# Column sums of three context blocks by accumulating transfers, in float16

## The chip, the core and the metric

The kernel runs on one core of a Trainium2 chip. The core has a matrix engine (TensorE, PE in the profile, with its weight loads as PEld), a vector engine (VectorE, DVE), a scalar engine (ScalarE, ACT), a general engine (GpSimd, POOL) and a queue engine (SyncE, SP). Each runs its own instructions in order, and they wait for each other by semaphores. Sixteen DMA engines move data between the device memory (DRAM), the on-chip buffers and, in this change, from one on-chip buffer to another; SP, ACT and POOL issue such transfers. The metric is the device time of one execution in microseconds (us), lower is better.

## The reference, cut to what matters

```python
# x: (2, 1024, 2048); ctx: (2, 2048, 2048)
def fake_quant(v, s, z):
    q = jnp.clip(jnp.round(v / s + z), 0, 255)
    return (q - z) * s

x = x + jnp.matmul(fake_quant(layernorm(x), s1, z1), fake_quant(ctx, s2, z2))
x = x + ffn(layernorm(x))     # x @ kernel + bias, and two low-rank adapters
```

The kernel keeps the quantised values as whole numbers less 128, which have eight significant bits, and multiplies those. The zero points z1 and z2 need not be 128, so the product has to be corrected by a term with the row sums of the first factor and by a term with the column sums of the second. The column sums of the context, 2048 rows added up for each of 2048 columns, are what this change is about.

## The kernel before, in words

The two batches are worked one after the other. In each, the context is taken in four blocks of 512 columns (n = 0 to 3), and x in four groups of 256 tokens (g = 0 to 3). A pair (b, n, g) is one block times one group: 2 halves of 128 tokens by 16 products of 128x128 by 128x512, accumulated in a bank of PSUM (class Pair, L513). Before its products a pair's bank is filled by ScalarE with the correction, from the block's column term colt[n] and the row sums (begin, L523); after them VectorE scales the bank into y (end, L545) and takes the statistics for the next norm (stats, L549, into st2).

A block's context arrives in eight slices of 256 rows. For each slice (quantise, L451) ScalarE rounds it to int16 (round_ctx, L455), and VectorE clips it, takes off 128 and writes it in two bytes an element into one of the two buffers of c2 (centre_ctx, L463). When all eight are there, column_term (L474) makes the block's column term: column_parts multiplies each of the sixteen 128-row pieces with a 128x32 matrix of ones, four lots of 32 rows of one PSUM tile (pcp), column_copy takes that to an on-chip buffer on VectorE, column_mean sums the 128 rows by one f32 product with a constant matrix (pc), and column_end turns it into colt on VectorE.

The first batch begins with an entry, in an order written out by hand (STEPS, in which u, p, c and v are the parts of the column term). It covers the products of blocks 0 and 1, and the making of block 2. Everything behind the entry is emitted in program order and put in order on each engine by a planner with its own costs. Block 3 of the first batch is quantised while block 2 is multiplied, and its column term is emitted after the third pair of block 2 (L1056 to L1064). In the second batch, blocks 0 and 1 are prepared inside the first batch's feed-forward part. Block 2 goes into the buffers of block 0 when the last pair of block 0 is done; it is quantised and summed while the last pair of block 1 runs (L1042 to L1049). Block 3 goes into the buffers of block 1 and is treated as in the first batch. Three buffers q2b pass the int16 slices from ScalarE to VectorE; ten buffers lit take the loads from DRAM, which SP issues as buffers come free.

After the attention part the adapters' matrices are gated (pg_a, pg_b), and the feed-forward part runs as a two-level fast matrix product with f32 operands on PE, with sums of operands on VectorE and POOL. POOL issues two transfers per batch (L679); the rest of its work is in the feed-forward part.

Of the kernel before, what the change touches and what calls it, by code (L numbers as in the profile page):

```python
# [9 lines left out]

F32 = mybir.dt.float32
BF16 = mybir.dt.bfloat16
U8 = mybir.dt.uint8
I16 = mybir.dt.int16
AF = mybir.ActivationFunctionType
ALU = mybir.AluOpType
# [4 lines left out]
P = 128  # L21
# [4 lines left out]
QMAX = 255.0  # L26
CENTRE = 128.0
# [52 lines left out]
EARLY = [(0, 0), (1, 0), (2, 0)]  # L80
ROWS_ON_SCALAR = ()
PLACED_BY_SCALAR = (2, 3, 4, 5, 6, 7)


class Bufs:
# [13 lines left out]
def tile_quant_xattn_then_lora_ffn(  # L99
# [17 lines left out]
    nc = tc.nc  # L117
# [28 lines left out]
    lit = Bufs([const.tile([P, KQ, GT], F32, tag=f"lit{i}", name=f"lit{i}") for i in range(10)])  # L146
    q2b = Bufs([const.tile([P, 2, NB], I16, tag=f"q2b{i}", name=f"q2b{i}") for i in range(3)])

    acat = const.tile([P, KT, GPB // 2 * 3, R], F32, tag="acat", name="acat")
    own_col = [0, 2, 3, 5]  # L150

# [2 lines left out]
    axT = const.tile([P, GPB // 2, GT], F32, tag="axT", name="axT")  # L154
    gmat = const.tile([P, 2, GPB // 2, RC], F32, tag="gmat", name="gmat")
    st1 = const.tile([P, MT, NN, 6], F32, tag="st1", name="st1")
    st2 = const.tile([P, MT, NN, 6], F32, tag="st2", name="st2")
    r_s = const.tile([P, MT], F32, tag="r_s", name="r_s")

    zs = [  # L160
# [6 lines left out]

    def bf(t, n):

        return t.rearrange("p k n -> p (k n)").bitcast(BF16).rearrange("p (k n) -> p k n", n=n)  # L170

    def flat(t):
        return t.rearrange("p k n -> p (k n)")
# [91 lines left out]
    load_x(0, 3)  # L265
    ahead[0] = 10
    load_next()
    gate_b = const.tile([P, GB, NL], F32, tag="gate_b", name="gate_b")
    nc.sync.dma_start(
        out=gate_b.rearrange("p b n -> p (b n)"), in_=gate.rearrange("b n -> (b n)").partition_broadcast(P)  # L270
    )
# [23 lines left out]

    ident = const.tile([P, P], F32, tag="ident", name="ident")
    make_identity(nc, ident)
    ident_h = const.tile([P, P], BF16, tag="ident_h", name="ident_h")
    nc.gpsimd.tensor_copy(ident_h, ident)
    ones_h = const.tile([P, P], BF16, tag="ones_h", name="ones_h")  # L300
    nc.gpsimd.memset(ones_h, 1.0)


    zeros_h = const.tile([P, P], BF16, tag="zeros_h", name="zeros_h")
    nc.gpsimd.memset(zeros_h, 0.0)
    mean_w = const.tile([P, P], F32, tag="mean_w", name="mean_w")
    nc.gpsimd.memset(mean_w, 1.0 / 32)

# [8 lines left out]

    def gate_values():

        m_ad = const.tile([P, NL], F32, tag="m_ad", name="m_ad")  # L320
        nc.vector.tensor_reduce(m_ad, ident.rearrange("p (n r) -> p n r", r=RC), AX.X, ALU.add)
        nc.vector.tensor_reduce(m_rk, ident.rearrange("p (n r) -> p r n", r=RC), AX.X, ALU.add)
        nc.vector.tensor_tensor(gate_b, gate_b, m_ad.unsqueeze(1).to_broadcast([P, GB, NL]), ALU.mult)
        for b in range(B):
            for i in range(2):
                nc.vector.tensor_reduce(
                    gval[:, ds(b * GPB + i * 2, 2)], gate_b[:, b * GPB + i : (b + 1) * GPB : 2, :], AX.X, ALU.add
                )
# [37 lines left out]
    class XTile:  # L366


        def __init__(self, b, m, c1T, wk):
            self.b, self.m, self.nm = b, m, f"{b}_{m}"  # L370
            self.on_vector = b == 0 and m not in ROWS_ON_SCALAR
            g, tok = m // MG, ds((m % MG) * P, P)
            self.y = y[g][:, m % MG, :]

            wf = flat(wk)
            self.q8 = wf[:, ds((m % 2) * (D // 4), D // 4)].bitcast(U8)
            self.qh = wf[:, D // 2 : D].bitcast(BF16)
            self.to = [c1T[g][:, ds(h * KH, KH), tok] for h in range(2)]
            self.pt = [None, None]

# [37 lines left out]
            )  # L418

        def turn(self, h):  # L420
            self.pt[h] = ps_m.tile([P, KH, P], BF16, tag="pm", name=f"pt_{self.nm}_{h}")
            for kt in range(KH):
                nc.tensor.transpose(self.pt[h][:, kt, :], self.qh[:, ds(h * H + kt * P, P)], ident_h)

# [23 lines left out]
            x.place(h)  # L448
        x.total()

    def quantise(c2, r):  # L451

        centre_ctx(c2, r, round_ctx())

    def round_ctx():  # L455
        buf, t = next_loaded(1)
# [3 lines left out]
        load_next()  # L460
        return qi

    def centre_ctx(c2, r, qi):  # L463
        nc.vector.tensor_scalar(c2[r // 4][:, ds(2 * (r % 4), 2), :], qi, QMAX, CENTRE, ALU.min, ALU.subtract)
        q2b.give(qi)

    def take_c2():
        bufs = [big.take() for _ in range(2)]
        return bufs, [bf(t, NB) for t in bufs]

    colt = {}
    pairs = []

    def column_term(b, n, c2):  # L474

        of = column_parts(b, n, c2)
        column_copy(of)
        column_mean(b, n, of)
        column_end(n, of)

    def column_parts(b, n, c2):

        parts = ps_m.tile([P, NB], F32, tag="pm", name=f"pcp_{b}_{n}")
        for k in range(KT):
            row = P // 4 * (k % 4)
            nc.tensor.matmul(
                parts[row : row + P // 4, :],
                ones_h[:, 0 : P // 4],
                c2[k // 8][:, k % 8, :],
                start=(k < 4),  # L490
                stop=(k >= KT - 4),
                skip_group_check=True,
            )
        return [parts]
# [18 lines left out]
    class Pair:  # L513
# [35 lines left out]
        def stats(self):  # L549
            for j in range(MG):  # L550
                nc.vector.bn_stats(  # L551
                    st2[:, self.g * MG + j, self.n, :], y[self.g][:, j, ds(self.n * NB, NB)]
                )

    def xattn_pair(b, n, g, c1T, c2):
# [66 lines left out]
    def prep_z(b, m, zq, wk):  # L622

        nm = f"{b}_{m}"
        g, tok = m // MG, ds((m % MG) * P, P)
        mean, rstd = norm_stats(st2[:, m], f"z{nm}")
        for h, t in enumerate(halves(wk)):
            nc.vector.tensor_scalar(t, y[g][:, m % MG, ds(h * H, H)], mean, rstd, ALU.subtract, ALU.mult)
            for u in range(2):
                pt = ps_m.tile([P, KQ, P], F32, tag="pm", name=f"ptz_{nm}_{h}_{u}")  # L630
                for k in range(KQ):
                    nc.tensor.transpose(pt[:, k, :], t[:, ds((4 * u + k) * P, P)], ident)  # L632
                nc.scalar.copy(zq[2 * h + u][:, :, tok], pt)
# [288 lines left out]
    def entry():  # L922

        X = [XTile(0, m, c1T, wk) for m in range(MT)]
        qi, parts, at, ad = {}, {}, {}, {}
        idle = ps_acc.tile([P, MG, NB], F32, tag="delta", name="idle")
        recent = [(idle, 0)]
        tick = const.tile([P, 1], BF16, tag="tick", name="tick")

        def pair(n, g):  # L930
            if (n, g) not in at:
# [1 line left out]
            return at[n, g]  # L933

        def products(n, g, j, first, last=None):
            recent.append((pair(n, g).pa, j))
            for r in range(first, (first if last is None else last) + 1):
                pair(n, g).products(j, range(2 * r, 2 * r + 2))

# [16 lines left out]
        def centred(r):  # L956
            if r // NR not in c2:
                next_block(0)
            centre_ctx(c2[r // NR], r % NR, qi.pop(r))

        def sums(n):
            parts[n] = column_parts(0, n, c2[n])

        def keep_busy(n):

            to, j = recent[-1]
            for i in range(n):
                nc.tensor.matmul(
                    to[:, j, :],
                    zeros_h,  # L970
                    (tick if to is idle else ones_h[:, 0:1]).to_broadcast([P, NB]),
                    start=(to is idle),
                    stop=True,
                    skip_group_check=True,
                )

        run = {
            "S": lambda m, n: X[m].stats(n),
# [9 lines left out]
            "Q": rounded,  # L988
            "V": centred,
            "u": sums,  # L990
            "p": lambda n: column_copy(parts[n]),
            "c": lambda n: column_mean(0, n, parts[n]),
            "v": lambda n: column_end(n, parts[n]),
            "B": lambda n, g, j: pair(n, g).begin(j),
            "M": products,
# [6 lines left out]
            "h": ad_copy,  # L1002
            "i": ad_turn,
            "j": lambda n: lora_a_place(n, ad[n]),
            "z": keep_busy,
        }
        for step in STEPS.split():
            done = run[step[0]](*(int(v) for v in step[1:].split(".") if v))
# [11 lines left out]
    for b in range(B):  # L1020
# [9 lines left out]
        else:  # L1030
# [5 lines left out]
            for g in range(2, GPB):  # L1036
                for m in range(g * MG, (g + 1) * MG):
                    with tc.issue_after(opened.ins):
                        prep_x(b, m, c1T, wk)
                for n in range(2):  # L1040
                    xattn_pair(b, n, g, c1T, c2[n])
                    if g + 1 == GPB:  # L1042
                        next_block(n)
                        if n == 0:
                            for r in range(NR):
                                quantise(c2[2], r)
                                if r % 4 == 3:
                                    lora_a_step(b, r // 4)
                            column_term(b, 2, c2[2])  # L1049
# [6 lines left out]
        for g in range(GPB):  # L1056
            if (b, g) != (0, 0):
                xattn_pair(b, 2, g, c1T, c2[2])
            for r in {0: range(3), 1: range(3, 6), 2: range(6, 8), 3: ()}[g]:
                quantise(c2[3], r)  # L1060
            if 1 <= g <= 2:
                lora_a_step(b, g + 1)
            if g == 2:
# [53 lines left out]
        def meanwhile(o, s):  # L1117
# [23 lines left out]
                load_x(nb, m, slice(half * H, (half + 1) * H))  # L1141
            if s < 4:
                for r in range(2 * s, 2 * s + 2):
                    quantise(c2[0], r)
            if 1 <= s <= 4:
                prep_x(nb, s - 1, state["c1T"], state["wk"])
            if s == 3:
# [2 lines left out]
                c2[1] = [bf(c2b[1][0], NB)]  # L1150
            if s == 4:
                for r in range(2):
                    quantise(c2[1], r)
                c2b[1].append(big.take())
                c2[1].append(bf(c2b[1][1], NB))
            if s == 5:
                for r in range(2, 5):
                    quantise(c2[1], r)
            if s == len(INNER) - 1:
                for r in range(5, NR):  # L1160
                    quantise(c2[1], r)
                column_term(nb, 1, c2[1])
                state["c1b"] += [big.take() for _ in range(2)]
                state["c1T"] = [bf(t, GT) for t in state["c1b"]]
# [59 lines left out]
```

## Time and profile before

| | |
|---|---|
| median of 3 runs | 1082.93 us (1082.42 to 1084.54) |
| the profiled execution | 1082.56 us, its span 1080.8 us |
| granted clock of PE | 1.00 |
| DVE, ACT and POOL busy | 71%, 23%, 23% of the span |
| DMA | 257.15 MB, 238 GB/s on average |
| the chain that ended last | PE 83%, DVE 8%, DMA 4%, ACT 3% |

Lines of the profile name an engine, a line of the kernel, an operation, and out<-in by the names of the tiles. L486 is the thin product of the column sums, L505 their f32 mean, L530 the products of a pair, L464 VectorE's write of a slice, L679 a transfer that POOL or ACT issues. An f32 product of the program is two records of PE. "DMA to landing" is the time from the start of the issuing instruction to the last of the 16 semaphore steps of its transfer. A DMA share of 1.00 means that the sixteen engines have packets in work all the time (it can come out a little above). The time in brackets behind an instruction is how long its engine was idle before it, and what ended that.

### The profile page before, as it was taken

How to read it: one execution, taken by the hardware profiler on the slowest of the kernel's cores; microseconds unless marked ns; L12 is line 12 of the kernel's file. 1: busy time of each engine (PE TensorE's matmuls, PEld its weight loads, DVE VectorE, ACT ScalarE, POOL GpSimd, SP SyncE). 2: the span in 40 equal slices, each digit the busy share in tenths (PEclk: the TensorE clock that was granted, in tenths of full speed). 3: DMA queues.
4: the chain of work that ended last, by engine and by line, in shares of the span. 5: the costliest groups of instructions: out<-in, count | busy, mean ns of one | idle time of the engine just before them, and what ended most of it. 6: DMA issues, size and time to landing. Idle time of an engine off the chain costs nothing.

```text
span 1080.8 us, 10609 instructions
## 1 busy us (share of the span) xinstructions
PE 1054.6 (98%) x3932; PEld 489.8 (45%) x3932; DVE 766.6 (71%) x949; ACT 247.4 (23%) x351; POOL 253.8 (23%) x104
## 2 busy tenths in 40 slices
PE   5999999999999999999999999999999999999998
PEld 2443345544444444444444444554444444444443
DVE  7986867578877676677859655674969667756851
ACT  5866133210000000001675741331000000000000
POOL 0000003032435302533000000032244531253600
PEclk9999999999999999999999999999999999999999
DMA  9979645788798476699673292559889874748611
GB/s 341 381 196 308 190 176 190 256 316 295 263 339 324 160 264 217 191 372 321 230 246 119 98 266 103 198 210 360 294 269 297 288 269 148 264 146 301 214 39 58
DMA packets 119228, 257.15 MB, mean 238 GB/s; under 512 B 11272, under 2 KB 15496, under 8 KB 118152
## 3 DMA queue, kind: packets, MB, share of 16 engines
q1 hardware_dynamic: 98688, 215.05, 58.4%
q10 hardware_dynamic: 20168, 40.38, 10.7%
q0 software_dynamic: 320, 1.05, 0.4%
q8 instruction: 31, 0.51, 0.2%
q14 instruction: 21, 0.17, 0.1%
HBM read 220.79 MB, written 37.75 MB: 239 GB/s over the span
## 4 chain that ended last, share of the span: by engine, by line
PE 83%; DVE 8%; DMA 4%; ACT 3%; issue 1%; SPq 0%; ACTq 0%
PE fu L828 34%; PE fv L828 17%; PE pa L530 12%; PE fw L828 9%; PE pl L694 3%; PE px L648 3%; PE ptz L632 2%; DMA lit<-in_ctx_dram 2%; DVE st L551 2%; DVE st L383 1%; ACT q2b L458 1%; DVE y L547 1%; ACT big L412 1%; DVE big L771 1%; PE pg_b L574 1%
## 5 line engine op out<-in xcount | busy, mean ns | idle before, releaser
L828 PE MATMUL fu<-big,lit 128*128 128x512 f32 x896 | 395.3, 593 | 0.0
L828 PEld LDWEIGHTS fu<-big,lit 128*128 128x128 f32 x896 | 168.6, 190 | 206.3 <-issue 204.9
L530 PE MATMUL pa<-big,big 128*128 128x512 bf16 x1024 | 237.1, 381 | 7.3 <-ACT pa L526 3.4
L771 POOL TENSOR_TENSOR lit<-lit,lit 128x1024 f32<-128x1024 f32 x56 | 164.7, 2950 | 189.7 <-PE fw L828 74.6
L828 PE MATMUL fv<-big,lit 128*128 128x512 f32 x448 | 197.9, 594 | 0.0
L771 DVE TENSOR_TENSOR big<-big,big 128x2048 f32<-128x2048 f32 x56 | 164.4, 2935 | 0.7
L530 PEld LDWEIGHTS <-big 128*128 128x128 bf16 x1024 | 97.1, 98 | 136.3 <-issue 29.6
L762 POOL TENSOR_TENSOR lit<-lit,lit 128x1024 f32<-128x1024 f32 x32 | 85.7, 2677 | 256.4 <-DMA lit<-zs 230.4
L852 DVE TENSOR_TENSOR y<-y,fu 128x1024 f32<-128x1024 f32 x92 | 108.5, 1215 | 40.6 <-PE fu L828 40.2
L828 PEld LDWEIGHTS fv<-big,lit 128*128 128x128 f32 x448 | 84.3, 190 | 105.0 <-issue 104.7
L458 ACT ACTIVATE q2b<-lit,sc,inv 128x1024 int16<-128x1024 f32 x64 | 76.4, 1232 | 163.7 <-DMA lit<-in_ctx_dram 147.1
L852 DVE TENSOR_TENSOR y<-y,fv 128x1024 f32<-128x1024 f32 x48 | 56.8, 1218 | 78.8 <-PE fv L828 78.8
L762 DVE TENSOR_TENSOR big<-big,big 128x2048 f32<-128x2048 f32 x40 | 101.8, 2546 | 0.0
L828 PE MATMUL fw<-big,lit 128*128 128x512 f32 x224 | 99.4, 592 | 0.0
L683 ACT COPY pl<-bias 128x1024 f32<-128x1024 f32 x16 | 16.3, 1018 | 294.1 <-DVE y L705 258.1
L679 POOL DMA_DIRECT2D bp<-bd x4 | 2.6, 660 | 344.3 <-DMA bd<-q2b 166.3
L852 DVE TENSOR_TENSOR y<-y,fw 128x1024 f32<-128x1024 f32 x24 | 28.4, 1218 | 53.9 <-PE fw L828 53.9
L828 PEld LDWEIGHTS fw<-big,lit 128*128 128x128 f32 x224 | 42.1, 190 | 50.7 <-issue 50.7
L547 DVE SCALAR_TENSOR_TENSOR y<-pa,k_s,y 128x1024 f32<-128x1024 f32 x32 | 41.0, 1280 | 32.2 <-PE pa L530 32.1
L526 ACT ACTIVATE pa<-bp,r_s 128x512 f32<-128x512 f32 x58 | 39.0, 685 | 87.0 <-PE pa L530 57.1
L705 DVE TENSOR_TENSOR y<-pl,y 128x512 f32<-128x512 f32 x64 | 39.8, 679 | 17.5 <-PE pl L694 17.2
L383 DVE BATCH_NORM_STATS2 st<-y 128x6 f32<-128x512 f32 x64 | 41.4, 679 | 5.7 <-DMA y<-in_x_dram 5.6
(93 smaller groups left out, 629.6 us busy)
## 6 DMA issues: line engine op xcount, KB each, us to landing
big<-in_w_dram SPq DMA_DIRECT2D x96, 1024.0 KB
lit<-zs SPq DMA_DIRECT2D x80, 512.0 KB
lit<-in_ctx_dram SPq DMA_DIRECT2D x64, 512.0 KB
out_dram<-y ACTq DMA_DIRECT2D x30, 512.0 KB
zs<-lit ACTq DMA_DIRECT2D x24, 512.0 KB
lit<-in_lora_a_dram SPq DMA_DIRECT2D x32, 256.0 KB
lit<-in_lora_bt_dram SPq DMA_DIRECT2D x32, 256.0 KB
y<-in_x_dram SPq DMA_DIRECT2D x16, 512.0 KB
```

Source lines behind the costliest of these rows:

```text
L383: nc.vector.bn_stats(st1[:, self.m, n, :], self.y[:, ds(n * NB, NB)])
L458: nc.scalar.activation(qi, t, AF.Relu, bias=z2, scale=inv2)
L526: nc.scalar.activation(self.pa[:, j, :], colt[self.n], AF.Identity, bias=r_s[:, m : m + 1])
L530: nc.tensor.matmul(self.pa[:, j, :], self.c1T[:, k, ds(j * P, P)], self.c2[k // 8][:, k % 8, :], start=not self.begun[j], stop=(k == KT - ...
L547: return nc.vector.scalar_tensor_tensor(yp, self.pa, s12, yp, ALU.mult, ALU.add)
L648: nc.tensor.matmul(px[i * 2 * R : (i + 1) * 2 * R, :], acat[:, k, ds(3 * pr + i, 2), :].rearrange("p s r -> p (s r)"), zqs[i][k // KQ][:, ...
L694: nc.tensor.matmul(pl[j][i][:, half], axT[rows, pr, ds(j * P, P)], bt[rows, half], start=False, stop=True, skip_group_check=True,)
L705: line(nc.vector.tensor_add(yb, pl[j][i], yb))
L762: line(eng.tensor_tensor(got[0], got[0], got[1], ALU.add if terms[1][2] > 0 else ALU.subtract))
L771: line(eng.tensor_tensor(out_t, at[p], at[q], op))
L828: nc.tensor.matmul(ps[m], at[:, k, ds(m * P, P)], bt[:, k, :], start=(opens and k == 0), stop=(ends and k == KQ - 1), skip_group_check=True,)
L852: line(nc.vector.tensor_tensor(yp, yp, whole[chain], op))
```

## The change: what it does

For three of the eight blocks, (b, n) = (0, 3), (1, 2) and (1, 3), the column sums are made in another way. After VectorE has written a slice, GpSimd issues a transfer of that slice (128 partitions x 1024 elements of two bytes, 256 KB) into a new buffer cs: a plain one for the first slice, accumulating ones for the other seven. There is one such buffer. When the eight are in, PE multiplies the two halves of cs with a 128x128 matrix of ones, two products 128x512 into one PSUM tile, and the column term follows from that as before. The sixteen thin products, the copy and the f32 mean of these three blocks are gone.

All two-byte tiles go from bfloat16 to float16, in which the sums of eight values are exact. To make room, the gate table and a small mask use the memory of cs before it is needed, and the second norm's statistics use the same tile as the first's (st1). A tile of zeros and a step that no order calls (keep_busy) are removed.

```diff
-BF16 = mybir.dt.bfloat16
+F16 = mybir.dt.float16
+SUMMED_BY_DMA = ((0, 3), (1, 2), (1, 3))
...
+    cs = Bufs([const.tile([P, 2, NB], F16, tag=f"cs{i}", name=f"cs{i}") for i in range(1)])
...
-    st2 = const.tile([P, MT, NN, 6], F32, tag="st2", name="st2")
...
-    gate_b = const.tile([P, GB, NL], F32, tag="gate_b", name="gate_b")
+    gate_b = cs.spare[0].rearrange("p k n -> p (k n)").bitcast(F32)[:, 0 : GB * NL].rearrange("p (b n) -> p b n", n=NL)
...
-    zeros_h = const.tile([P, P], BF16, tag="zeros_h", name="zeros_h")
-    nc.gpsimd.memset(zeros_h, 0.0)
...
-    def centre_ctx(c2, r, qi):
-        nc.vector.tensor_scalar(c2[r // 4][:, ds(2 * (r % 4), 2), :], qi, QMAX, CENTRE, ALU.min, ALU.subtract)
+    def centre_ctx(b, n, r, qi):
+        part = c2[n][r // 4][:, ds(2 * (r % 4), 2), :]
+        nc.vector.tensor_scalar(part, qi, QMAX, CENTRE, ALU.min, ALU.subtract)
         q2b.give(qi)
+        if (b, n) in SUMMED_BY_DMA:
+            if r == 0:
+                slices[n] = cs.take()
+                nc.gpsimd.dma_start(out=slices[n], in_=part)
+            else:
+                nc.gpsimd.dma_start(out=slices[n], in_=part, accum_op=ALU.add)
...
     def column_term(b, n, c2):
         of = column_parts(b, n, c2)
-        column_copy(of)
-        column_mean(b, n, of)
+        if (b, n) not in SUMMED_BY_DMA:
+            column_copy(of)
+            column_mean(b, n, of)
         column_end(n, of)
 
     def column_parts(b, n, c2):
+        if (b, n) in SUMMED_BY_DMA:
+            pc = ps_m.tile([P, NB], F32, tag="pm", name=f"pc_{b}_{n}")
+            for i in range(2):
+                nc.tensor.matmul(pc, ones_h, slices[n][:, i, :], start=(i == 0), stop=(i == 1))
+            cs.give(slices.pop(n))
+            return [pc]
...
-                    st2[:, self.g * MG + j, self.n, :], y[self.g][:, j, ds(self.n * NB, NB)]
+                    st1[:, self.g * MG + j, self.n, :], y[self.g][:, j, ds(self.n * NB, NB)]
```

More of the change, by code (lines that the diff above doesn't have):

```diff
@@ L168, in bf @@
     def bf(t, n):
-        return t.rearrange("p k n -> p (k n)").bitcast(BF16).rearrange("p (k n) -> p k n", n=n)
+        return t.rearrange("p k n -> p (k n)").bitcast(F16).rearrange("p (k n) -> p k n", n=n)
     def flat(t):
@@ L297, in tile_quant_xattn_then_lora_ffn @@
     make_identity(nc, ident)
-    ident_h = const.tile([P, P], BF16, tag="ident_h", name="ident_h")
+    ident_h = const.tile([P, P], F16, tag="ident_h", name="ident_h")
     nc.gpsimd.tensor_copy(ident_h, ident)
-    ones_h = const.tile([P, P], BF16, tag="ones_h", name="ones_h")
+    ones_h = const.tile([P, P], F16, tag="ones_h", name="ones_h")
     nc.gpsimd.memset(ones_h, 1.0)
-    zeros_h = const.tile([P, P], BF16, tag="zeros_h", name="zeros_h")
-    nc.gpsimd.memset(zeros_h, 0.0)
     mean_w = const.tile([P, P], F32, tag="mean_w", name="mean_w")
@@ L318, in gate_values @@
     def gate_values():
-        m_ad = const.tile([P, NL], F32, tag="m_ad", name="m_ad")
+        m_ad = cs.spare[0].rearrange("p k n -> p (k n)").bitcast(F32)[:, ds(GB * NL, NL)]
         nc.vector.tensor_reduce(m_ad, ident.rearrange("p (n r) -> p n r", r=RC), AX.X, ALU.add)
@@ L376, in __init__ @@
             self.q8 = wf[:, ds((m % 2) * (D // 4), D // 4)].bitcast(U8)
-            self.qh = wf[:, D // 2 : D].bitcast(BF16)
+            self.qh = wf[:, D // 2 : D].bitcast(F16)
             self.to = [c1T[g][:, ds(h * KH, KH), tok] for h in range(2)]
@@ L420, in turn @@
         def turn(self, h):
-            self.pt[h] = ps_m.tile([P, KH, P], BF16, tag="pm", name=f"pt_{self.nm}_{h}")
+            self.pt[h] = ps_m.tile([P, KH, P], F16, tag="pm", name=f"pt_{self.nm}_{h}")
             for kt in range(KH):
@@ L449, in prep_x, with quantise @@
         x.total()
-    def quantise(c2, r):
-        centre_ctx(c2, r, round_ctx())
+    def quantise(b, n, r):
+        centre_ctx(b, n, r, round_ctx())
     def round_ctx():
@@ L471, in tile_quant_xattn_then_lora_ffn @@
     colt = {}
+    slices = {}
     pairs = []
@@ L625, in prep_z @@
         g, tok = m // MG, ds((m % MG) * P, P)
-        mean, rstd = norm_stats(st2[:, m], f"z{nm}")
+        mean, rstd = norm_stats(st1[:, m], f"z{nm}")
         for h, t in enumerate(halves(wk)):
@@ L925, in entry @@
         qi, parts, at, ad = {}, {}, {}, {}
-        idle = ps_acc.tile([P, MG, NB], F32, tag="delta", name="idle")
-        recent = [(idle, 0)]
-        tick = const.tile([P, 1], BF16, tag="tick", name="tick")
+        tick = const.tile([P, 1], F16, tag="tick", name="tick")
         def pair(n, g):
@@ L935, in products @@
         def products(n, g, j, first, last=None):
-            recent.append((pair(n, g).pa, j))
             for r in range(first, (first if last is None else last) + 1):
@@ L958, in centred @@
                 next_block(0)
-            centre_ctx(c2[r // NR], r % NR, qi.pop(r))
+            centre_ctx(0, r // NR, r % NR, qi.pop(r))
         def sums(n):
             parts[n] = column_parts(0, n, c2[n])
[L964 to L975, printed above, removed]
         run = {
@@ L990, in entry @@
             "u": sums,
-            "p": lambda n: column_copy(parts[n]),
-            "c": lambda n: column_mean(0, n, parts[n]),
+            "p": lambda n: (0, n) in SUMMED_BY_DMA or column_copy(parts[n]),
+            "c": lambda n: (0, n) in SUMMED_BY_DMA or column_mean(0, n, parts[n]),
             "v": lambda n: column_end(n, parts[n]),
@@ L1004, in entry @@
             "j": lambda n: lora_a_place(n, ad[n]),
-            "z": keep_busy,
         }
@@ L1045, in tile_quant_xattn_then_lora_ffn @@
                             for r in range(NR):
-                                quantise(c2[2], r)
+                                quantise(b, 2, r)
                                 if r % 4 == 3:
@@ L1059, in tile_quant_xattn_then_lora_ffn @@
             for r in {0: range(3), 1: range(3, 6), 2: range(6, 8), 3: ()}[g]:
-                quantise(c2[3], r)
+                quantise(b, 3, r)
             if 1 <= g <= 2:
@@ L1143, in meanwhile @@
                 for r in range(2 * s, 2 * s + 2):
-                    quantise(c2[0], r)
+                    quantise(nb, 0, r)
             if 1 <= s <= 4:
@@ L1152, in meanwhile @@
                 for r in range(2):
-                    quantise(c2[1], r)
+                    quantise(nb, 1, r)
                 c2b[1].append(big.take())
@@ L1157, in meanwhile @@
                 for r in range(2, 5):
-                    quantise(c2[1], r)
+                    quantise(nb, 1, r)
             if s == len(INNER) - 1:
                 for r in range(5, NR):
-                    quantise(c2[1], r)
+                    quantise(nb, 1, r)
                 column_term(nb, 1, c2[1])
```

## The prediction

> **What bounds the kernel now.** I read the page first, then TensorE (PE) in order of time where the three changed blocks are summed, then the engines that feed it, and last the only transfers that GpSimd (POOL) issues.
>
> ```profile
> span 1080.8 us, 10609 instructions
> PE 1054.6 (98%) x3932; PEld 489.8 (45%) x3932; DVE 766.6 (71%) x949; ACT 247.4 (23%) x351; POOL 253.8 (23%) x104
> ```
>
> PE is busy in 98% of the span and carries 83% of the chain that ended last. So work taken off PE is time gained, and a wait put in front of PE is time lost, one for one. Now the order of PE in the second batch, where block 2 is summed (columns: start, duration, engine, line, operation, count):
>
> ```profile
> 616.62 3.63 PE L530 MATMUL pa<-big,big 128*128 128x512 bf16 x16
> 620.30 0.63 PE L600 MATMUL pga<-ident,q2b 128*128 128x128 f32 x4
> 620.86 1.05 PE L486 MATMUL pcp<-big,ones_h 128*32 128x512 bf16 x16
> 621.84 1.04 PE L530 MATMUL pa<-big,big 128*128 128x512 bf16 x4
> 622.71 1.12 PE L505 MATMUL pc<-q2b,mean_w 128*128 128x512 f32 x2
> 623.67 7.50 PE L530 MATMUL pa<-big,big 128*128 128x512 bf16 x34
> ```
>
> The sixteen thin products (pcp) and the f32 mean (pc) lie in an unbroken row of products; nothing there waits. When the data comes is seen on VectorE (DVE), whose writes at L464 put the eight slices of block 2 in place:
>
> ```profile
> 612.27 0.86 DVE L464 TENSOR_SCALAR big<-q2b 128x1024 bf16<-128x1024 int16 x2 [1.61 <-PE pa L530]
> ...
> 618.47 1.08 DVE L464 TENSOR_SCALAR big<-q2b 128x1024 bf16<-128x1024 int16 x3
> ...
> 620.19 0.43 DVE L464 TENSOR_SCALAR big<-q2b 128x1024 bf16<-128x1024 int16 x1
> ```
>
> The last slice is ready at 620.6, and PE sums at 620.86: hardly any slack. The first slice is ready at 612.7 and cannot be earlier, since it overwrites a buffer that PE has just finished with. The nearest row to the new transfers is bp<-bd, the four DMAs that POOL issues, of 256 KB each, which is also the size of one slice:
>
> ```profile
> L679 POOL DMA_DIRECT2D bp<-bd x1: 686/686/686, 153.8 to 153.8; - x1
> ...
> DMA to landing us min/median/max: 6.9/6.9/6.9
> ...
> L679 POOL DMA_DIRECT2D bp<-bd x1: 852/852/852, 167.4 to 167.4; - x1
> ...
> DMA to landing us min/median/max: 3.9/3.9/3.9
> ...
> DMA to landing us min/median/max: 7.1/7.1/7.1
> ...
> DMA to landing us min/median/max: 4.2/4.2/4.2
> ```
>
> The four answers are in order of time (issued at 153.8, 167.4, 684.2, 698.2). Stretches of the trace (span; sum; PE, PEld, DVE, ACT, POOL; clock; DMA share; GB/s) tell why they differ:
>
> ```profile
> 154.00:161.00 7.00, 7.00 (x38) 2.71 (x36) 3.71 (x10) 1.19 (x4) 0.47 (x1) 1.00 0.97 360
> 168.00:172.00 4.00, 4.00 (x28) 2.40 (x28) 2.04 (x6) 2.16 (x4) 0.25 (x1) 1.00 0.70 220
> ...
> 108.00:121.00 13.00, 12.60 (x63) 5.42 (x62) 13.00 (x24) 0.94 (x2) 0.00 (x0) 1.00 1.04 270
> ...
> 620.00:650.00 30.00, 29.72 (x156) 12.70 (x155) 15.88 (x31) 14.53 (x17) 0.00 (x0) 1.00 1.02 263
> 650.00:660.00 10.00, 10.00 (x62) 4.14 (x61) 5.36 (x10) 1.91 (x3) 0.00 (x0) 1.00 0.02 5
> ```
>
> The third was issued at a share of 1.03, the fourth at 0.53 (stretches 683 to 685 and 697 to 699). With the DMA engines full at the issue a POOL transfer took 7.0 us, otherwise 4.05 (means of two each). The stretches that matter are full: 94 to 121 (block 3 of the first batch) and 614 to 650 (blocks 2 and 3 of the second).
>
> **The change part by part.**
>
> *Taken off PE.* Per block the sixteen thin products take 0.98 us (620.86 to 621.84) and the f32 mean 0.96, 0.96 and 0.86 in the three places (to the next start): together 5.7. Added are two products 128x512, 0.22 each (a row of 32 takes 7.01): 1.3. Gain 4.4 us, all on PE's path. The three copies of 0.69 us leave DVE, which has idle time there: nothing.
>
> *The chain of transfers.* A block has one plain transfer and seven accumulating ones, all into the single buffer cs. In the built program each waits for the semaphore of the one before, so eight times issue-to-landing lie end to end, and PE's two products wait for the last. PE is in order; behind them stand the adapter product pg_a or the running pair, and every pair that needs this column sum. POOL has no other work there (0.00 busy in those stretches), so nothing else is late on it; SP's loads of adapters, which wait for buffers that pg_a frees, are used only behind the same wait. The bounds of one link: below, the trace excludes nothing down to POOL's own issue (0.54 to 0.85 us in the four rows); above, 8.1 full and 5.15 light, if reading the destination doubles the transfer itself, which for queue 0 is 0.4% of the span for four, 1.1 us each. I take 7.0 and 4.05: same issuer, same size, with a plain copy's HBM trip standing in for the second read.
>
> *Second batch, block 2.* Without the old sums PE does 0.56 of pga from 620.30 and sixteen products (3.5), and is at the two products at 624.4. Links: 612.7 to 616.75 light (the loads only start again at 613), five full ones to 651.75, two light ones to 659.85. The loads do not stop with PE: the sixteen rounded slices free their buffers on ScalarE, without PE. Wait 659.85 - 624.4 = 35.4. After it the sum is turned into the bias (DVE 0.81, ACT 0.69, about 1.4 from product to bias, as from 655.35 to 656.7 in this trace) with only pg_a (1.0) in front of the pair: 0.4 more.
>
> *Second batch, block 3.* Its slices are ready by then, but its first transfer stands on POOL behind the other block's and needs cs, so it starts when PE has read cs, 660.3. Eight light links end 32.4 later. PE gets there 24.6 after (24.2 from 626.3 to 650.53 now, and the 0.4): wait 7.8.
>
> *First batch, block 3.* First slice ready at 94.1, four full links to 122.1, four light ones to 138.3; the last slice is written only at 122.46, behind DVE's statistics, and does not decide. PE arrives at 126.2 (pga at 125.20, then two products): wait 12.1. Loads and weights that run meanwhile are waited for by nobody earlier than now.
>
> *The clock after a wait.* The trace has one idle stretch of this kind, 8.0 us before 13.14, and the products after it:
>
> ```profile
> 16.39 1.89 PE L530 MATMUL pa<-big,big 128*128 128x512 bf16 x4 [2.22 <-DVE big L428]
> ...
> 30.41 1.02 PE L530 MATMUL pa<-big,big 128*128 128x512 bf16 x4 [0.23 <-DVE big L464]
> ```
>
> The same four products took 1.89 and later 1.02. Two groups of four and two of eight transposes lost 0.87, 0.72, 0.41 and 0.44 against their later rows: 2.4 us before the pace was reached (bounds: 0, and 2.4). The granted clock says 1.00 all through, so it does not show this. Three waits of about 8 us or more: 7.2.
>
> *Priced at nothing.* float16 for bfloat16 has the same two bytes; the rows that come nearest, bf16 products at 0.22 and weights at 98 ns (f32: 190), I take over. The other end, the f32 product's 0.88, would add hundreds of us and is not credible. The gate table in cs is long used by 94. st1 in place of st2 adds order only among DVE's own instructions, which are in order. zeros_h is a 0.20 us memset on POOL at 1.42, 11 us ahead of the first transpose. keep_busy is called by no step.
>
> *Sum.* 35.4 + 0.4 + 7.8 + 12.1 + 7.2 - 4.4 = +58.5, against this execution's own 1082.56 (span 1080.8), which is 0.4 below the median of 1082.93. Forecast 1141.
>
> *The skill against the rows.* The Trainium skill, "DMA: Bandwidth & Descriptors" (Anatomy of one DMA), puts a transfer from GpSimd at about 2.0 us plus the bytes over 436 GB/s, which makes an estimate of 2.6 us for 256 KB. The four rows of this trace show 3.9 to 7.1, so the rows decide; with 2.6 a link only block 2 of the second batch would wait, and the time would be some 1090. "TensorE: Matmul & The Clock Gate" (Part 1) says that an idle window of about 3.4 us halves the array's clock until as long a busy one has passed. That speaks against a change that makes PE wait; the products after 13.14 agree, and by the page each wait would cost an estimated 1.7 us, the sum being 2 us lower.
>
> **The rivals.**
>
> *A: the queue is no matter.* Without HBM at either end every link takes 4.05. Then 94.1 + 32.4 ends with the last slice (122.9 + 4.05), wait 0.8; block 2 waits until 645.1, 20.7; block 3 7.8; two slow starts 4.8: +30, 1113. For it: the light rows. Against: 6.9 and 7.1 whenever the engines were full.
>
> *B: the second read costs.* 8.1 and 5.15 a link: waits of 20.9, 41.3 and 16.6, in all +82, 1165. For it: twice the bytes are read. Against: no HBM trip.
>
> *C: faster.* The accumulating transfers from buffer to buffer are short. With a link of L, block 2 waits 8L - 11.7; with 0.4 and the gain of 4.4 the balance is at L = 1.96. At 1.46 or less no wait is left, and the time is 1079. For it: PE's gain is real, and no row shows such a transfer. Against: the shortest of four rows is 3.9.
>
> *D: the transfers are hidden in part.* Links of 2.5 to 3.2 give +6 to +13, 1089 to 1096, all of it from block 2 of the second batch.
>
> **How the numbers follow.** A measurement of this kernel tells about 0.2% (2 us) from no change. Forecast 48%, A 22%, B 18%, D 6%, C 4%, and 2% for a link close to 1.96, within 0.2%. Faster 0.04, same 0.02, slower 0.94. The range takes in A (down to links of about 3.8, less slow starts) and reaches past B's 1165: 1104 to 1168; outside it lie C, D and the far side of B.
>
> **What would show it.** On PE, two waits for a DMA of cs before pc in the second batch, 35 and 8 us, and one of 12 in the first; on POOL, 24 transfers, each issued when the one before landed, 7 us apart before 650 and 4 after; on PE 48 records fewer (per block 18 go and 2 come). Products just after the long wait near 0.43 us each. It is wrong if links are shorter than 3.5 us while the engines are full, or if the float16 products are not at 0.22.

## The result, and the profile after

The changed kernel takes 1144.68 us (median of 4 runs, 1141.6 to 1146.71) against 1083.74 before (4 runs). The ratio is 1.0555, with a 95% interval of 1.0522 to 1.0589: it is 61 us slower. The forecast was 1141. The profiled execution took 1141.6 us, its span 1139.7; it is the fastest of the four, 3.1 us below their median, and everything read from the trace below is of this execution.

The page of the kernel after, first lines and the row of TensorE's granted clock:

```profile
span 1139.7 us, 10576 instructions
...
PE 1056.9 (93%) x3884; PEld 489.7 (43%) x3884; DVE 762.8 (67%) x946; ACT 247.7 (22%) x351; POOL 268.5 (24%) x127
...
PEclk9999799999999999999999758999999999999999
...
q0 software_dynamic: 3584, 7.34, 3.3%
```

PE has 48 records fewer, as forecast. PE's busy time does not fall with them (1056.9 us, 1054.6 before), because some of the others now run at a lower clock: the slices where the clock row dips are the ones that hold the three waits. The transfers of GpSimd's queue (q0) are 6.3 MB more than before, 2% of all bytes.

PE in order of time around the three sums, in the kernel after (start, duration, engine, line, operation, count, idle time before):

```profile
139.62 1.04 PE L494 MATMUL pc<-cs,ones_h 128*128 128x512 f16 x2 [14.36 <-DMA cs<-big]
140.45 3.71 PE L544 MATMUL pa<-big,big 128*128 128x512 f16 x12
...
673.29 1.03 PE L494 MATMUL pc<-cs,ones_h 128*128 128x512 f16 x2 [35.16 <-DMA cs<-big]
674.25 1.94 PE L588 MATMUL pg_a<-lit,gmat 128*32 128x512 f32 x8
676.12 11.66 PE L544 MATMUL pa<-big,big 128*128 128x512 f16 x48
...
707.24 1.03 PE L494 MATMUL pc<-cs,ones_h 128*128 128x512 f16 x2 [7.06 <-DMA cs<-big]
708.07 5.76 PE L544 MATMUL pa<-big,big 128*128 128x512 f16 x16
```

The three waits are 14.4, 35.2 and 7.1 us, 56.6 together. Behind each wait the products are slow for a while: the twelve from 140.45 take until 144.09 where 2.63 us is their usual time, the sixteen from 708.07 take until 713.76, 5.7 us instead of 3.5. In the stretch from 707 to 714 PE's granted clock is 0.61. Against the usual times (0.22 us for a product, 1.0 for pg_a) the rows shown lose 1.4, 2.35 and 2.6 us, 6.3 in all. So 56.6 - 4.4 + 6.3 = 58.5, and the spans differ by 58.9. Nothing is given back later: the adapters' products px of the second batch start at 699.8 before and at 758.7 after, 58.9 later, and that difference stays to the end.

The chain itself, on POOL, second batch:

```profile
626.48 0.56 POOL L469 DMA_DIRECT2D cs<-big  x1 [95.38 <-DVE big L464]
632.45 0.90 POOL L471 DMA_DIRECT2D cs<-big  x1 [5.41 <-DVE big L464]
641.58 0.87 POOL L471 DMA_DIRECT2D cs<-big  x1 [8.24 <-DVE big L464]
650.32 0.86 POOL L471 DMA_DIRECT2D cs<-big  x1 [7.87 <-DMA lit<-in_lora_bt_dram]
658.48 0.86 POOL L471 DMA_DIRECT2D cs<-big  x1 [7.30 <-issue]
662.26 0.87 POOL L471 DMA_DIRECT2D cs<-big  x1 [2.92 <-DMA cs<-big]
...
674.62 0.57 POOL L469 DMA_DIRECT2D cs<-big  x1 [3.84 <-PE pc L494]
677.46 0.86 POOL L471 DMA_DIRECT2D cs<-big  x1 [2.27 <-DVE q2b L604]
684.32 0.86 POOL L471 DMA_DIRECT2D cs<-big  x1 [6.00 <-DMA cs<-big]
```

From issue to issue an accumulating link of block 2 takes 8.2 to 9.1 us until 658, then 3.8. (The releasers named are those of the last semaphore that came; the slices were there long before, the last of block 2 at 634.1.) Three stretches of the same kernel (span; sum; PE, PEld, DVE, ACT, POOL; clock; DMA share; GB/s), the second of which lies within the first, show what changes at 658:

```profile
627.00:658.00 31.00, 10.96 (x57) 4.67 (x54) 12.71 (x30) 15.21 (x14) 2.67 (x4) 0.72 1.05 298
650.30:658.50 8.20, 0.00 (x0) 0.00 (x0) 0.00 (x0) 0.00 (x0) 0.88 (x2) 0.50 1.01 280
658.00:674.00 16.00, 0.71 (x2) 0.13 (x2) 0.00 (x0) 0.00 (x0) 3.48 (x4) 0.50 0.40 72
```

The DMA engines are full up to 658 and at 0.40 after it. From 650.3 to 673 PE, VectorE and ScalarE do nothing, with PE's clock granted at half. The link from 650.32 to 658.48 took 8.2 us all the same, and those behind it 3.8: so the length of a link does not come from what VectorE or ScalarE do beside it.

### The profile page after: what moved, and what is told of

The parts are those of the page before. It is cut to its first block, busy times and chain, and to the rows that moved or that the text cites. A ratio compares the mean times of both kernels' runs of the same rounds, so it can differ in the third digit from the quotient of the medians.

```text
span 1139.7 us, 10576 instructions
## 1 busy us (share of the span) xinstructions
PE 1056.9 (93%) x3884; PEld 489.7 (43%) x3884; DVE 762.8 (67%) x946; ACT 247.7 (22%) x351; POOL 268.5 (24%) x127
## 5 line engine op out<-in xcount | busy, mean ns | idle before, releaser
L544 PE MATMUL pa<-big,big 128*128 128x512 f16 x1024 | 240.6, 386 | 6.6 <-ACT pa L540 2.8
L785 POOL TENSOR_TENSOR lit<-lit,lit 128x1024 f32<-128x1024 f32 x56 | 162.8, 2917 | 188.0 <-PE fw L842 60.0
L544 PEld LDWEIGHTS <-big 128*128 128x128 f16 x1024 | 98.5, 99 | 138.3 <-issue 33.6
L776 POOL TENSOR_TENSOR lit<-lit,lit 128x1024 f32<-128x1024 f32 x32 | 82.5, 2580 | 263.3 <-DMA lit<-zs 237.7
L494 PE MATMUL pc<-cs,ones_h 128*128 128x512 f16 x6 | 3.1, 620 | 56.6 <-DMA cs<-big 56.6
```

Source lines behind the costliest of these rows:

```text
L544: nc.tensor.matmul(self.pa[:, j, :], self.c1T[:, k, ds(j * P, P)], self.c2[k // 8][:, k % 8, :], start=not self.begun[j], stop=(k == KT - ...
L776: line(eng.tensor_tensor(got[0], got[0], got[1], ALU.add if terms[1][2] > 0 else ALU.subtract))
L785: line(eng.tensor_tensor(out_t, at[p], at[q], op))
```

## The experiments

**Theory.** The loss is PE standing in front of two products that wait for eight transfers end to end, and a transfer is long because the DMA engines are full. **Rivals:** float16 or the shared tiles cost something; the accumulation is what is slow; a link's length is its own, whatever else is transferred; the bytes are too many for the DMA engines; the blocks hinder each other through the one buffer.

### The types and shared tiles alone

```diff
-SUMMED_BY_DMA = ((0, 3), (1, 2), (1, 3))
+SUMMED_BY_DMA = ()
```

> Only the types change: all eight blocks are summed by PE's thin products again, in float16, with st1 and the shared memory as in the changed kernel. My theory (the cost is the wait for the chains of transfers): no difference from the kernel before, 1083.7 within 2 us. Rival (float16 itself, or the shared tiles, cost something): a visible part of the 61 us stays.

Measured: 1082.71 us (10 runs) against 1083.31 (13 runs), ratio 0.9997, interval 0.9986 to 1.0009. So float16, the shared statistics tile, the gate table's new place and the removed tile cost nothing that can be measured. All 61 us lie in the transfers and what waits for them.

### One block at a time

```diff
-SUMMED_BY_DMA = ((0, 3), (1, 2), (1, 3))
+SUMMED_BY_DMA = ((0, 3),)
```

> Only block 3 of the first batch is summed by transfers. Theory of the serial chain: the wait of 14 us before its two products stays as it is, less the 1.5 us of sums saved, plus 1 to 2 us at the lower clock: 1097 to 1099. Rival (the three chains hinder each other, or a cost that does not belong to a block): well under 1095, or over 1102.

Measured: 1099.64 us (one run), a wait of 15.8. That is 0.6 us over the range that was given. In this execution the wait came out 1.4 us longer than in the kernel after, and the twelve products behind it took 5.1 us instead of the 3.6 there.

```diff
-SUMMED_BY_DMA = ((0, 3), (1, 2), (1, 3))
+SUMMED_BY_DMA = ((1, 3),)
```

> Only block 3 of the second batch is summed by transfers. Theory of the serial chain that is slow where the DMA engines are full: the chain now starts with the first slice, about 623, has four links of 6 to 8.5 us until about 654 and four of 3.8, ends about 669, and PE is there at about 650: a wait of 17 to 21 us, longer than the 7 us with all three blocks, and 1100 to 1105 in all. Rival (block 3 waits only because its chain stands behind block 2's and there is one buffer): no wait, 1082 to 1083.

Measured: 1102.68 us (one run). In this kernel the first six transfers of POOL's chain, with the answer on PE's wait:

```profile
623.50 0.57 POOL L469 DMA_DIRECT2D cs<-big  x1 [105.30 <-DVE big L464]
632.28 0.91 POOL L471 DMA_DIRECT2D cs<-big  x1 [8.21 <-DMA cs<-big]
640.54 0.88 POOL L471 DMA_DIRECT2D cs<-big  x1 [7.35 <-DMA cs<-big]
648.86 0.86 POOL L471 DMA_DIRECT2D cs<-big  x1 [7.44 <-DMA cs<-big]
654.13 0.87 POOL L471 DMA_DIRECT2D cs<-big  x1 [4.40 <-DVE acat L620]
657.98 0.87 POOL L471 DMA_DIRECT2D cs<-big  x1 [2.98 <-DMA cs<-big]
```

```profile
PE pc L494 <- DMA cs<-big: 18.2, 1, 18.2
```

The rival falls: with block 2 out of the way and the buffer free, block 3 waits 18.2 us, not none and not 7.1. Alone, its chain starts in the full stretch (8.3 to 8.8 us a link up to 649); behind block 2's, it starts when PE has already stood for 35 us, and only its second link (6.9 us) meets many loads. The short wait of 7.1 in the kernel after was paid for in the long one.

### Copies in place of accumulation

```diff
-                nc.gpsimd.dma_start(out=slices[n], in_=part, accum_op=ALU.add)
+                nc.gpsimd.dma_start(out=slices[n], in_=part)
```

> All 24 transfers are plain copies into the same buffer; the sums of the three blocks are left out, the last slice stands for them. Theory (what costs is eight round trips end to end, each as long as the DMA engines are full): links of about 7 to 8 us where they are full and 2.8 otherwise, waits of about 10, 31 and 1 us, 1128 to 1132. Rival (the accumulation is what is slow): links of 3 us and less everywhere, waits of 0, 10 and 0 us, about 1090.

Measured: 1127.75 us (one run), 0.25 under the range that was given; waits of 44.6 us in all, the longest 33.6. From issue to landing, for the 21 transfers at L471 of this kernel, and after it the same answer for the kernel after:

```profile
DMA to landing us min/median/max: 2.2/2.7/7.9
```

```profile
DMA to landing us min/median/max: 3.2/3.3/8.6
```

The accumulation costs about 1 us a transfer where the engines are quiet (the shortest of each: 3.2 and 2.2), and 0.7 between the longest of each, which lie in full stretches. A plain copy, with no device memory at either end, also takes up to 7.9 us. So most of the length in a full stretch is not the addition's.

### Without the loads beside it

```diff
+        if b == 1:
+            left_out.append(len(todo))
...
+            taken[0] += 1
...
-            if len(srcs) == 1:
+            if taken[0] > left_out[0]:
+                pass
+            elif len(srcs) == 1:
                 nc.sync.dma_start(out=t, in_=srcs[0])
```

Here taken counts the entries of the list of loads that have been reached, and left_out holds the number of those up to block 1 of the second batch.

> The changed kernel without the loads of the second batch's context blocks 2 and 3 and of its adapters: what the buffers held before is worked on instead, so the output of the second batch is not the reference's. Theory (a link is long because the DMA engines are full with these loads): in the second batch every link takes 2.8 (copy) or 3.8 us, block 2's chain takes about 29 us instead of 46.8 and its wait 17 instead of 35; the other waits stay near 14 and 7: 1125 to 1129. Rival (a link's length is its own, or lies with VectorE or POOL): 1142 to 1146.

Measured: 1124.57 us (one run), 0.4 under the range that was given. The first transfers of block 2's chain on POOL, a stretch, and PE's wait, in this kernel:

```profile
630.16 0.56 POOL L476 DMA_DIRECT2D cs<-big  x1 [95.02 <-DVE big L471]
633.03 0.90 POOL L478 DMA_DIRECT2D cs<-big  x1 [2.31 <-DMA cs<-big]
636.88 0.99 POOL L478 DMA_DIRECT2D cs<-big  x1 [2.95 <-DVE big L471]
641.14 0.97 POOL L478 DMA_DIRECT2D cs<-big  x1 [3.27 <-DVE big L471]
645.02 0.86 POOL L478 DMA_DIRECT2D cs<-big  x1 [2.91 <-DVE st L572]
```

```profile
627.00:655.00 28.00, 14.65 (x77) 5.93 (x74) 14.74 (x35) 16.56 (x15) 6.02 (x7) 0.81 0.33 63
```

```profile
PE pc L501 <- DMA cs<-big: 37.2, 3, 18.1
```

The copy's link is 2.9 us and the others 3.8 to 4.3, although VectorE and ScalarE work beside them as before. Only the loads are gone. The longest wait is 18.1 instead of 35.2, the others are 15.7 and 3.4, and the time is 20 us below the median of the changed kernel (17 below its profiled execution). This shows the second half of the theory: the accumulating links of block 2 are about twice as long (8.7 us on the mean of three, 4.0 here) because the loads run beside them. What within the queues makes it so was not tried, and a share of 1.0 alone does not fix the length: in the first batch of the kernel after, one accumulating link took 5.8 us at a share of 1.03, and the next 8.2:

```profile
102.62 0.91 POOL L471 DMA_DIRECT2D cs<-big  x1 [8.03 <-DVE pa L557]
108.46 0.88 POOL L471 DMA_DIRECT2D cs<-big  x1 [4.94 <-DMA cs<-big]
116.67 0.86 POOL L471 DMA_DIRECT2D cs<-big  x1 [7.33 <-DMA cs<-big]
```

### Two chains side by side

```diff
+    cs.give(axT.rearrange("p a t -> p (a t)").bitcast(F16).rearrange("p (k n) -> p k n", n=NB))
...
-            if r == 0:
-                slices[n] = cs.take()
-                nc.gpsimd.dma_start(out=slices[n], in_=part)
+            if r < 2:
+                slices.setdefault(n, []).append(cs.take())
+                nc.gpsimd.dma_start(out=slices[n][r], in_=part)
             else:
-                nc.gpsimd.dma_start(out=slices[n], in_=part, accum_op=ALU.add)
+                nc.gpsimd.dma_start(out=slices[n][r % 2], in_=part, accum_op=ALU.add)
...
-            for i in range(2):
-                nc.tensor.matmul(pc, ones_h, slices[n][:, i, :], start=(i == 0), stop=(i == 1))
+            for i in range(4):
+                nc.tensor.matmul(pc, ones_h, slices[n][i // 2][:, i % 2, :], start=(i == 0), stop=(i == 3))
...
```

The second buffer is the memory of axT, which nothing else uses while these blocks are summed.

> Two chains of four transfers each (even and odd slices, two buffers, four products with ones instead of two) in place of one of eight. Theory (a link is waiting, two can wait side by side): about four links end to end, waits of 0 to 3, 17 to 20 and 0 us instead of 14, 35 and 7, 1100 to 1106. Rival (the DMA engines' throughput for these bytes sets the chain): two side by side take twice as long, 1140 to 1146.

Measured: 1113.05 us (one run). On POOL and on PE's wait, in this kernel:

```profile
626.62 0.90 POOL L472 DMA_DIRECT2D cs<-big  x1 [4.79 <-DVE big L465]
629.04 0.88 POOL L472 DMA_DIRECT2D axT<-big  x1 [1.52 <-DMA axT<-big]
634.86 0.86 POOL L472 DMA_DIRECT2D cs<-big  x1 [4.94 <-DVE st L567]
637.40 0.86 POOL L472 DMA_DIRECT2D axT<-big  x1 [1.67 <-DMA axT<-big]
643.27 0.86 POOL L472 DMA_DIRECT2D cs<-big  x1 [5.01 <-DMA cs<-big]
```

```profile
PE pc L495 <- DMA cs<-big: 21.7, 2, 18.9
```

A link of one chain takes 8.2 to 8.4 us here too (626.62 to 634.86, to 643.27), with the other chain's link inside the same time. So here the length of a link is not the throughput of the DMA engines for its bytes, since twice as many pass in the same time, and half as many links end to end halve the long wait: 18.9, as expected; the others are 2.8 us and, in block 3, none. The time is 7 us above the range, though. PE in order of time behind the long wait:

```profile
651.08 1.03 PE L495 MATMUL pc<-cs,ones_h 128*128 128x512 f16 x2 [18.91 <-DMA cs<-big]
652.04 1.94 PE L590 MATMUL pg_a<-lit,gmat 128*32 128x512 f32 x8
653.91 1.03 PE L495 MATMUL pc<-axT,ones_h 128*128 128x512 f16 x2
656.57 12.34 PE L546 MATMUL pa<-big,big 128*128 128x512 f16 x48 [1.63 <-ACT pa L542]
```

The span is 30.5 us longer than before. Waits for transfers make 21.7 of that and 0.3 for the second buffer; the pair's products wait 1.6 for their correction after block 2's sum; the rows behind the two waits lose 6.3 against their usual times; and ahead of block 2's sum in the second batch (520 to 620) PE waits 2.0 longer for ScalarE than before (3.6 and 1.6). The gain is 3.1 here, as each block has two further products (1.3 us for three). That makes 28.8; the other 1.7 stay open, and so does why ScalarE is later.

### The sum used late

Block 2 of the second batch goes back to PE. The two blocks 3 keep two chains, and their sum comes after the first pair of block 3, whose correction VectorE adds afterwards.

```diff
-SUMMED_BY_DMA = ((0, 3), (1, 2), (1, 3))
+SUMMED_BY_DMA = ((0, 3), (1, 3))
...
-    def xattn_pair(b, n, g, c1T, c2):
-        p = Pair(b, n, g, c1T, c2)
+    def xattn_pair(b, n, g, c1T, c2, term=None):
+        p = Pair(b, n, g, c1T, c2, begun=term is None)
...
+        if term is not None:
+            term()
+            for j in range(MG):
+                p.late(j)
         summed = p.end()
...
-            if g == 2:
-                column_term(b, 3, c2[3])
...
-            xattn_pair(b, 3, g, c1T, c2[3])
+            xattn_pair(b, 3, g, c1T, c2[3], (lambda: column_term(b, 3, c2[3])) if g == 0 else None)
```

> Block 2 of the second batch is summed by PE as before; the two blocks 3 by two chains of four, and their sum is used late: the first pair of block 3 is multiplied without the correction, then come PE's four products with ones, then VectorE adds the correction to that pair. So PE comes to the products some 12 to 15 us later. Theory (all of the loss is PE's standing in front of the transfers): no wait for a transfer is left, and the time is the kernel before less 2 x 1.06 us: 1080 to 1082.5. Rival (the transfers or the late correction cost in another way, for instance VectorE or the loads): over 1085.

The control has the same edits with all sums by PE:

```diff
-SUMMED_BY_DMA = ((0, 3), (1, 3))
+SUMMED_BY_DMA = ()
```

> As the kernel with late use, but with all sums by PE: the late use alone. Theory: it neither saves nor costs, 1083 within 1.5 us, so that what the kernel with late use and transfers saves against this one is the two blocks' sums, 2.1 us. Rival: the late use costs or saves more than 2 us by itself.

Measured: 1088.82 us (6 runs) with the transfers and 1090.93 (5 runs) without, against 1082.98 before (11 runs); ratios 1.0061 (1.0049 to 1.0073) and 1.0083 (1.0070 to 1.0096). PE's waits, first in the kernel with the transfers, then in the control:

```profile
PE ptz L653 <- ACT lit L654: 3.1, 1, 3.1
...
PE pg_b L595 <- DVE bp L527: 1.4, 1, 1.4
```

```profile
PE ptz L653 <- ACT lit L654: 3.1, 1, 3.1
PE pc L521 <- DVE q2b L515: 2.8, 2, 2.0
```

In the kernel with transfers no wait for a transfer is left on PE in the profiled execution, which is the fastest of the six (1085.29). By the medians it takes 2.1 us less than its control, which is what was expected of the two blocks' sums; but the two intervals overlap, so a gain is not shown, only that the transfers of two blocks, which made PE wait 15.8 and 18.2 us when summed early, no longer cost time that can be measured. Both expectations about the late use fail: it costs 8 us by itself, and the time with transfers is over 6 us above the range given. Of the 8, 5.9 are two groups of waits in the control that the kernel before does not have, 3.1 of the transposes for ScalarE (also there with the transfers) and 2.8 of the mean for VectorE's copy; behind the 3.1 the next rows lose about 1.4 more. The rest was not traced. No kernel tried beats the one before.

## Why the prediction was right

The forecast, 1141, is 0.6 us below the profiled execution and 3.7 below the median. The mechanism held: three waits for the chains in front of PE, slow products behind them, less the gain. That the total came so close is in part luck, since the errors of the terms have both signs: the waits came out 2.3 longer, 0.2 shorter and 0.7 shorter, the slow products 0.9 less, and 0.4 did not show.

- **PE's gain of 4.4 us**: the balance of the span closes with it to 0.4 us, and 48 records are gone. Float16 at bfloat16's price held (0.9997).
- **The chains**: waits of 12.1, 35.4 and 7.8 were forecast and 14.4, 35.2 and 7.1 measured. Their links were not those of the working. I took 7.0 us for a link in the full stretch and 4.05 in the quiet one from the four POOL transfers of before; measured were mostly 8.2 to 9.1 and 3.8. In the first batch the chain took 45.7 instead of 44.2, and PE stood in front of it 0.9 earlier. In block 2 of the second batch the first link was put as quiet, and took 6.0. Then four links, not six, ran before the loads were through, so longer links and fewer of them made nearly the same end, 46.8 us where 47.2 were forecast. That the 35.2 is so close is luck: its links were not.
- **Block 3 of the second batch**: all eight links were forecast as quiet, 32.4 us. The first, a copy, took 2.8 and the second, beside loads, 6.9; the sum is 32.6, again close by luck. PE got there 25.6 us after the chain began, not 24.6.
- **The slow products after a wait**: 7.2 forecast, 6.3 measured. The prediction had only the slow rows at the start, where the granted clock still reads 1.00. Here the clock itself is in the profile, 0.50 from 658 to 674 and 0.61 in the stretch with the sixteen slow products. The Trainium skill, "TensorE: Matmul & The Clock Gate" (Part 1), gives half the rate after an idle window, and an estimate from it was 1.7 us a wait; the three places show 1.4, 2.35 and 2.6, so the sum lies between that estimate and the forecast.
- **The 0.4 us** for turning the sum into the bias did not show: pg_a, itself slow for 1.9 us, covers it.
- **The rivals.** A (the queue does not matter without HBM at either end) falls by the copies, 7.9 us from buffer to buffer, and by the kernel without the loads. B had the full link right at 8.1 and the quiet one too high at 5.15. C would have needed links under 1.96, and D links of 2.5 to 3.2; the shortest accumulating transfer landed after 3.2, and none was followed by the next within 3.5. (By its own terms D's sum is 6.7 to 13.3 us, of which 1.0 at the upper end comes from block 3.)
- The Trainium skill's line in "DMA: Bandwidth & Descriptors" (Anatomy of one DMA), an estimate of 2.6 us for 256 KB, lies near the copy that met quiet engines, 2.3 us to landing; beside full ones the same transfer took up to 8.2 here.

## What to carry to other kernels

Work moved from a busy engine to chained transfers is paid in round trips: count them end to end, price each by the stretch it runs in and not by the bytes, and compare the sum with the time from the first input, when the chain can start, to the consumer's place in its queue (here 11.7 us for block 2, against a chain of 46.8). A few microseconds of matrix work are cheap against eight such trips. Removing one wait can lengthen another: look at when a chain starts and what else fills the DMA engines at that time.

## What had not been expected of the hardware

- A copy of 256 KB from one on-chip buffer to another, issued by GpSimd, lands after 2.2 to 2.3 us beside quiet DMA engines and, one at a time, after up to 8.2 beside full ones. Accumulating adds 1 us to the first and little to the second (up to 8.6 in the kernel after).
- Two such transfers in flight each take as long as one alone, 8.2 to 8.4 us from issue to issue, in a stretch where the DMA share is already 1.04.
- Block 3's wait was longer by itself (18.2 us) than with block 2's chain in front of it (7.1).
